# Second attention of a two-layer block: scores in two orientations instead of transposed exponentials

## The chip, the cores and the metric

The kernel runs on one core of a Trainium2 chip. The metric is device time in microseconds (us) of one execution; the time of a kernel is the median of its runs.

## What is computed

The block holds 16 sequences of 128 tokens with 256 features and runs two layers on them: a quantized attention, a gated feed-forward part (FFN), a second attention, and a mixture of experts (MoE). The change touches the second attention alone:

```
def _L1_xattn_ref(Q, K, V, attention_mask, w_q, w_k, w_v, w_o, b_o):
    q = (Q @ w_q.T).reshape(B, S, G, HG, HD)      # 8 groups x 4 heads, head size 8
    k = (K @ w_k.T).reshape(B, S, G, HD)
    v = (V @ w_v.T).reshape(B, S, G, HD)
    scores = jnp.einsum('bnghd,bmgd->bnghm', q, k) / scale
    scores = jnp.where(pad, NEG_INF, scores)      # masked keys
    scores = jnp.where(causal, scores, NEG_INF)   # keys after the query
    attn = jax.nn.softmax(scores, axis=-1)
    out = jnp.einsum('bnghm,bmgd->bnghd', attn, v).reshape(B, S, D)
    return out @ w_o.T + b_o
```

There are 32 heads of size 8; four heads share one key and value head. Softmax is taken with the row's maximum subtracted.

## The kernel before

The layers run one after the other, with some overlap at their borders. The second attention is the loop at the end of the listing below. It starts while the FFN's last four sequences are still being written (`down`), and it interleaves four kinds of side work: the input side of the next four sequences (`front_step`: load, normalize, transpose with `turn`, project with `qk`), `keys`, the output projection `output`, and the routing of finished tokens to experts (`route`, a generator of which each step runs one stage). The tile framework orders the instructions of each engine by dependency and priority, so side work lands between the attention's own instructions.

A step n of that loop handles one sequence b, one half c of the 256 features (16 heads) and one pair p of 32-row strips (8 heads). 64 steps make the stage; two steps with the same b and c are called a **pass** here, and there are 32 passes.

- `keys(b)`: GpSimd copies the keys four times, each copy zeroed except for the eight rows of one head (`kb`, line 975). The value heads are spread over 32-column slots (`vpad`, line 986).
- `scores(n)`: two matmuls with an identity put the mask into PSUM (line 997, bf16), and two matmuls of 32 rows each, one in each of two row strips of the array, add queries times keys (line 1004). The result has queries on partitions.
- `top(n)`: VectorE takes minus the maximum over the keys (line 1011).
- `exp(n)`: ScalarE takes eight exponentials of 128 x 128, one for each head, as the maximum is a bias per partition and differs between heads (line 1020).
- `probs(n)`: the values product contracts over keys, which must be on partitions. So TensorE transposes the exponentials (line 1031), and VectorE copies them out of PSUM (line 1032).
- `values(n)`, once per pass: 16 matmuls with the values and 16 with ones for the row sums (line 1047), each in one of four 32-column strips of the array; a reciprocal and a product on VectorE (lines 1053, 1054) give the output.

[...] Before, the stage has two score tiles of two banks, two banks for transposes (tag `tr`), one for everything else (tag `mm`: projections, `keys`, `output`, `down`, routing) and one for `values` (tag `pv`).

Of the kernel before, what the change touches and what calls it, by code (L numbers as in the profile page):

```python
# [9 lines left out]
F32 = mybir.dt.float32  # L10
# [3 lines left out]
I32 = mybir.dt.int32  # L14
AF = mybir.ActivationFunctionType
ALU = mybir.AluOpType
AX = mybir.AxisListType

P = 128
B = 16  # L20
# [15 lines left out]
def flamingo_kernel(  # L36
# [40 lines left out]
    def ps(tag, shape, bufs):  # L77
        return psum.tile(shape, F32, tag=tag, name=f"ps_{tag}", bufs=bufs)

    def ps_mm(shape):  # L80
        return ps("mm", shape, 2)

    def ps_tr(shape):
        return ps("tr", shape, 2)

    def ps_sc(shape):
        return ps("sc", shape, 2)
# [14 lines left out]
    def kpn(ap):  # L102
        return ap.rearrange("(k p) n -> p k n", p=P)
# [135 lines left out]
    with (  # L239
# [74 lines left out]
        class Unit:  # L314
# [198 lines left out]
            def probs(self, c):  # L513
                e, _ = self.e.pop(c)
                pt = ps_tr([P, 4, P])
                for j in range(4):
                    nc.tensor.transpose(pt[:, j, :], e[:, j, :], ident)  # L517
                eT = ap.tile([P, 4, P], F32, tag="eT", name="eT")
                nc.scalar.copy(eT, pt)  # L519
                self.eT[c] = eT  # L520
# [343 lines left out]
    ao = cq.tile([P, KD, DM], F32, name="ao")  # L864
    bo = cq.tile([P, DM], F32, name="bo")
    nc.sync.dma_start(out=aq, in_=kpn(aqT))
    nc.sync.dma_start(out=ak, in_=kpn(akT))
    nc.sync.dma_start(out=av, in_=kpn(avT))
    nc.sync.dma_start(out=ao, in_=kpn(aoT))
    nc.sync.dma_start(out=bo, in_=b_o.partition_broadcast(P))  # L870
# [8 lines left out]
        base=0, channel_multiplier=1,  # L879
    )  # L880

    hmask = cq.tile([P, NQ], F32, name="hmask")
    nc.vector.memset(hmask, 0.0)
    for q in range(P // 32):
        rows = hmask[32 * q : 32 * q + 32, :]
        nc.gpsimd.memset(rows, 1.0)
        nc.gpsimd.affine_select(
            out=rows, in_=rows, pattern=[[-HD, NQ]], compare_op=ALU.is_ge, fill=0.0,
            base=0, channel_multiplier=1,
        )  # L890
        nc.gpsimd.affine_select(
            out=rows, in_=rows, pattern=[[HD, NQ]], compare_op=ALU.is_ge, fill=0.0,
            base=HD - 1, channel_multiplier=-1,
        )

    ones8 = cq.tile([P, NQ, 32], F32, name="ones8")
    vpads = [cq.tile([P, NG, NQ, 32], F32, name=f"vpad{i}") for i in range(2)]
# [41 lines left out]
    def turn(g):  # L939
        y = front[g]["y"]  # L940
        hT = gp.tile([P, KD, NT], F32, tag="hT", name="hT", bufs=1)
        for k in range(KD):
            pt = psum.tile([P, G, P], F32, tag="tr", name="ps_tr", bufs=2)
            for j in range(G):
                nc.tensor.transpose(pt[:, j, :], y[:, j, k * P : (k + 1) * P], ident)
            nc.scalar.copy(hT[:, k, :], pt.rearrange("p n t -> p (n t)"))
        front[g]["hT"] = hT

    def qk(g, i, c):

        f = front[g]
        if c == 0:
            f[i] = gp.tile([P, KD, NT], F32, tag="qk"[i], name="qk"[i] + "T")
        w, src = ((aq, f["hT"]), (ak, f["cT"]))[i]
        pm = psum.tile([P, NT], F32, tag="mm", name="ps_mm")
        for k in range(KD):
            nc.tensor.matmul(
                pm, w[:, k, c * P : (c + 1) * P], src[:, k, :],
                start=(k == 0), stop=(k == KD - 1),
            )  # L960
        if i == 0:
            nc.scalar.activation(f[i][:, c, :], pm, AF.Copy, scale=SCALE1)
        else:
            nc.scalar.copy(f[i][:, c, :], pm)

    kbs, vps, es, eTs, oTs, scs, mxs = {}, {}, {}, {}, {}, {}, {}

    def keys(b):

        g, j = divmod(b, G)  # L970
        f = front[g]
        tok = slice(j * P, (j + 1) * P)
        kb = ap.tile([P, KD, NQ, P], F32, tag="kb", name="kb")
        for c in range(KD):
            nc.gpsimd.tensor_tensor(  # L975
                kb[:, c], f[1][:, c, None, tok].to_broadcast([P, NQ, P]),
                hmask[:, :, None].to_broadcast([P, NQ, P]), ALU.mult,
            )
        pm = psum.tile([P, NG, HD], F32, tag="mm", name="ps_mm")
        for k in range(KD):  # L980
            nc.tensor.matmul(
                pm, f["cT"][:, k, tok], av[:, k, :], start=(k == 0), stop=(k == KD - 1)
            )
        vp = vpads[b % 2]
        for i in range(NQ):
            nc.vector.tensor_copy(vp[:, :, i, HD * i : HD * i + HD], pm)
        kbs[b], vps[b] = kb, vp

    def scores(n):

        b, c, p = n // 4, n // 2 % 2, n % 2
        g, j = divmod(b, G)
        f = front[g]
        tok = slice(j * P, (j + 1) * P)
        s = psum.tile([P, 2, NQ, P], F32, tag="sc", name="ps_sc", bufs=2)
        for i in range(2):
            nc.tensor.matmul(
                s[:, i], identb, f["comb"][:, j, None, :].to_broadcast([P, NQ, P]),
                start=True, stop=False,
            )  # L1000
        with tc.high_priority(offset=100):
            for i in range(2):
                rows = slice(32 * (2 * p + i), 32 * (2 * p + i) + 32)
                nc.tensor.matmul(  # L1004
                    s[:, i], f[0][rows, c, tok], kbs[b][rows, c], start=False, stop=True
                )
        scs[n] = s

    def top(n):
        mx = small.tile([P, 8], F32, tag="mx8", name="mx8")  # L1010
        nc.vector.tensor_reduce(  # L1011
            mx, scs[n].rearrange("p i h t -> p (i h) t"), AX.X, ALU.max, negate=True
        )
        mxs[n] = mx

    def exp(n):
        s, mx = scs.pop(n), mxs.pop(n)
        e = ap.tile([P, 8, P], F32, tag="e", name="e", bufs=3)
        for i in range(8):
            nc.scalar.activation(  # L1020
                e[:, i, :], s[:, i // NQ, i % NQ, :], AF.Exp, bias=mx[:, i : i + 1]
            )
        es[n] = e

    def probs(n):
        e = es.pop(n)
        eT = ap.tile([P, 2, NQ, P], F32, tag="eT", name="eT", bufs=3)
        for i in range(2):
            pt = psum.tile([P, NQ, P], F32, tag="tr", name="ps_tr", bufs=2)
            for h in range(NQ):  # L1030
                nc.tensor.transpose(pt[:, h, :], e[:, NQ * i + h, :], ident)
            nc.vector.tensor_copy(eT[:, i], pt)
        eTs[n] = eT

    def values(n):

        if n % 2 == 0:
            return
        b, c = n // 4, n // 2 % 2
        if c == 0:  # L1040
            oTs[b] = ap.tile([P, KD, P], F32, tag="oT", name="oT")
        o = psum.tile([P, 2, P], F32, tag="pv", name="ps_pv", bufs=1)
        for t in range(2):
            for h in range(NQ):
                for q in range(4):
                    lhs = ones8[:, h, :] if t else vps[b][:, 4 * c + q, h, :]
                    nc.tensor.matmul(
                        o[32 * q : 32 * q + 32, t, :], lhs,
                        eTs[n - 1 + q // 2][:, q % 2, h, :],
                        start=(h == 0), stop=(h == NQ - 1),  # L1050
                    )
        r = ap.tile([P, P], F32, tag="rsum", name="rsum")
        nc.vector.reciprocal(r, o[:, 1, :])
        nc.vector.tensor_tensor(oTs[b][:, c, :], o[:, 0, :], r, ALU.mult)
# [29 lines left out]
    for g in range(B // G):  # L1084
# [3 lines left out]
        for b in range(g * G, (g + 1) * G):  # L1088
            down(b, hd, ps_pv([P, DM]) if b % 2 else ps_acc([P, DM]))
            if g == 1:  # L1090
                for i in range(3 * (b % G), 3 * (b % G) + 3):
                    front_step(0, i)
    psum0.close()
    act_set = nc.scalar.preload_act_table_set("natural_log_exp_and_others")
    tc.keep_in_program_order(act_set)
    f2 = ExitStack()
# [5 lines left out]
    )  # L1102


    N1 = 4 * B
    routes = []
    for n in range(-2, N1 + 5):
        if 0 <= n < N1:
            scores(n)
            top(n)  # L1110
        if 0 <= n - 1 < N1:
            probs(n - 1)
        if 0 <= n < N1:
            exp(n)
        if 0 <= n < G:
            down(B - G + n, hd, psum.tile([P, DM], F32, tag="mm", name="ps_mm"))
            if n == G - 1:
                tp.close()
                ep = ctx.enter_context(tc.tile_pool(name="e1", bufs=2, reuse_waits="tile"))
        if 0 <= n - 2 < N1:  # L1120
            values(n - 2)
        m = n + 2
        if m % 4 == 0 and 0 <= m < N1:
            keys(m // 4)
        g, i = divmod(n + 12, 16)
        if 1 <= g < B // G:
            front_step(g, i)
        for stages in routes:
            next(stages, None)
        m = n - 4  # L1130
        if m % 4 == 3 and 0 <= m < N1:
            output(m // 4)
            for b0, count in ROUTES:
                if m // 4 == b0 + count - 1:
                    routes.append(route(b0, count))
    for stages in routes:
        for _ in stages:
            pass
    f2.close()
    f1.close()  # L1140

    psum = ctx.enter_context(
        tc.tile_pool(
# [123 lines left out]
```

## Time and profile before

| | |
|---|---|
| median of 3 runs | 1544.2 us (1540.3 to 1545.12) |
| the profiled execution: time | 1540.11 us |
| the profiled execution: span of the trace | 1538.2 us |
| its mean granted TensorE clock | 0.968 |
| second attention, first mask matmul to last values matmul | about 1080 to 1389 us |
| first matmul of the MoE | 1411.87 us |

The profile gives, for each engine, its busy time; PE is TensorE's matmuls, PEld its weight loads, DVE is VectorE, ACT is ScalarE, POOL is GpSimd and SP issues DMAs. A matmul of fp32 data stands in the trace as two records, a transpose or a bf16 matmul as one. Records of matmuls overlap, since a new one starts while an earlier one drains, so the distance between the starts tells the cost and the duration of a record does not. Names such as L1004 are lines of the kernel before.

### The profile page before, as it was taken

The page shows a single profiled execution, that of the slowest core. Times are in us where ns is not written, and L with a number is a line of the kernel's source. Part 1 is how long each engine was busy: PE and PEld are TensorE (multiplying, and loading weights), DVE is VectorE, ACT ScalarE, POOL GpSimd, SP SyncE. Part 2 cuts the span into 40 slices and gives each one's busy share as a digit, 9 for nine tenths or more (in the row PEclk, how much of TensorE's full clock was granted, in tenths as well). Part 3 has the DMA queues.
Part 4 walks back from the last instruction along what each step waited for, and adds up shares of the span by engine and source line. Part 5 has one row for each costly group of instructions (what it writes and reads, how often), then busy time and mean ns, then how long its engine had stood idle before and what let it go on. Part 6 is the DMA issues. An engine that isn't in the chain of part 4 may idle for free. (4 is left out here: it accounts for less than half of the span.)

```text
span 1538.2 us, 24640 instructions
## 1 busy us (share of the span) xinstructions
PE 1388.1 (90%) x8612; PEld 1009.7 (66%) x8612; DVE 1052.2 (68%) x2788; ACT 814.6 (53%) x2421; POOL 669.5 (44%) x574
## 2 busy tenths in 40 slices
PE   2778889798897999999999986999999999996998
PEld 1567677677675677777777764555556666664887
DVE  8888878878789777676767765433579797883100
ACT  3656566566556676666666662353355454542121
POOL 4576666666766555556565554120021312111111
PEclk9799999999999999999999998999999999996999
DMA  4300000000013100000000003400210100001662
GB/s 122 112 7 18 28 11 32 15 11 22 11 45 100 44 23 22 11 19 15 18 15 18 8 8 110 141 1 0 83 49 9 50 9 36 9 36 63 194 198 67
DMA packets 51115, 68.67 MB, mean 45 GB/s; under 512 B 5291, under 2 KB 37739, under 8 KB 50992
## 3 DMA queue, kind: packets, MB, share of 16 engines
q1 hardware_dynamic: 36912, 41.31, 9.1%
q10 hardware_dynamic: 11456, 17.63, 3.6%
q0 software_dynamic: 2624, 8.16, 1.5%
q8 instruction: 68, 1.11, 0.3%
q14 instruction: 55, 0.45, 0.1%
HBM read 50.53 MB, written 16.81 MB: 44 GB/s over the span
## 5 line engine op out<-in xcount | busy, mean ns | idle before, releaser
L509 POOL TENSOR_TENSOR e<-e,sums 128x512 f32<-128x512 f32 x128 | 139.7, 1092 | 230.8 <-DVE sums L505 120.8
L497 ACT ACTIVATE e<-ps_sc,mx 128x128 f32<-128x128 f32 x512 | 181.3, 368 | 90.1 <-DVE mx L489 82.7
L454 POOL TENSOR_TENSOR raw<-raw,q_r 128x512 f32<-128x512 f32 x192 | 207.9, 1112 | 34.1 <-DVE q_r L180 33.0
L431 DVE BATCH_NORM_STATS2 q_st<-raw 128x6 f32<-128x128 f32 x768 | 174.1, 279 | 66.9 <-ACT raw L422 66.5
L1020 ACT ACTIVATE e<-ps_sc,mx 128x128 f32<-128x128 f32 x512 | 139.7, 384 | 119.1 <-DVE mx L1011 114.1
L565 PE MATMUL ps_acc<-wp,cat 128*128 128x512 f32 x512 | 160.4, 436 | 17.6 <-POOL cat L227 15.5
L463 PE MATMUL ps_tr<-ident,raw 128*128 128x128 f32 x768 | 121.9, 288 | 46.0 <-POOL raw L454 43.8
L227 POOL TENSOR_TENSOR cat<-e_t,e_e 128x1024 fp32r<-128x1024 bf16 x64 | 136.2, 2128 | 53.7 <-DVE e_t L221 52.1
L481 PE MATMUL ps_sc<-kT,qT 128*128 128x128 f32 x1024 | 140.3, 280 | 15.0 <-ACT qT L472 15.0
L481 PEld LDWEIGHTS ps_sc<-kT,qT 128*128 128x128 f32 x1024 | 131.1, 193 | 33.0 <-ACT qT L472 27.0
L463 PEld LDWEIGHTS ps_tr<-ident,raw 128*128 128x128 f32 x768 | 96.0, 147 | 83.3 <-POOL raw L454 58.2
L519 ACT COPY eT<-ps_tr 128x512 f32<-128x512 f32 x128 | 75.4, 589 | 139.0 <-PE ps_tr L517 138.9
L975 POOL TENSOR_TENSOR kb<-kT,hmask 128x512 f32<-128x512 f32 x32 | 33.6, 1067 | 243.9 <-PE ps_sc L1004 184.6
L565 PEld LDWEIGHTS ps_acc<-wp,cat 128*128 128x128 f32 x512 | 95.9, 194 | 57.4 <-POOL cat L227 22.2
L527 PE MATMUL ps_pv<-eT,vt 128*128 128x256 f32 x512 | 132.1, 379 | 1.0 <-DVE cat_y L538 1.0
L422 ACT COPY raw<-ps_mm 128x512 f32<-128x512 f32 x192 | 113.7, 593 | 27.9 <-PE ps_mm L410 24.8
L527 PEld LDWEIGHTS ps_pv<-eT,vt 128*128 128x128 f32 x512 | 95.9, 189 | 31.2 <-issue 9.0
L538 DVE TENSOR_TENSOR cat_y<-ps_pv,r_sm 128x512 bf16<-128x512 f32 x128 | 87.1, 680 | 39.7 <-PE ps_pv L527 39.5
L472 ACT ACTIVATE qT<-ps_tr,hv 128x512 f32<-128x512 f32 x128 | 100.9, 789 | 21.8 <-PE ps_tr L463 19.8
L497 ACT ACTIVATION_READ_ACCUMULATOR e<-ps_sc,mx 128x1 f32 x512 | 105.3, 206 | 0.0
L489 DVE TENSOR_REDUCE mx<-ps_sc 128x4 f32<-128x512 f32 x128 | 87.2, 681 | 23.6 <-PE ps_sc L481 23.6
L1011 DVE TENSOR_REDUCE mx<-ps_sc 128x8 f32<-128x1024 f32 x64 | 78.2, 1222 | 25.0 <-PE ps_sc L1004 23.4
(228 smaller groups left out, 2807.3 us busy)
## 6 DMA issues: line engine op xcount, KB each, us to landing
w1t<-in_w ACTq DMA_DIRECT2D x8, 1024.0 KB, 5.0
w2t<-in_w ACTq DMA_DIRECT2D x8, 1024.0 KB, 5.6
disp<-empty SPq DMA_DIRECT2D x16, 257.0 KB, 8.5
xe<-disp SPq DMA_DIRECT2D x8, 514.0 KB, 3.6
stage<-in_wprojT SPq DMA_DIRECT2D x16, 256.0 KB, 2.7
xg<-in_x SPq DMA_DIRECT2D x4, 512.0 KB, 3.9
xb<-in_x SPq DMA_DIRECT2D x16, 128.0 KB, 2.1
ctx<-in_ctxT SPq DMA_DIRECT2D x16, 128.0 KB, 2.2
```

The costliest lines, as they stand in the source:

```text
L227: nc.gpsimd.tensor_tensor(dst, t[:, part], e[:, part], ALU.subtract)
L422: nc.scalar.copy(raw.rearrange("p h d -> p (h d)"), pm)
L431: nc.vector.bn_stats(self.st[:, 4 * blk + j, :], self.raws[blk][:, j, :])
L454: nc.gpsimd.tensor_tensor(src, src, self.r[:, 4 * blk : 4 * blk + 4, None].to_broadcast([P, 4, P]), ALU.mult,)
L463: nc.tensor.transpose(pt[:, j, :], src[:, j, :], ident)
L472: nc.scalar.activation(dst, pt, AF.Identity, scale=hv[:, col : col + 1], bias=hv[:, col + 1 : col + 2])
L481: nc.tensor.matmul(pscore[:, j, :], qT[:, j, :], self.kT[:, 2 * c + j // 2, :], start=True, stop=True,)
L497: nc.scalar.activation(e[:, j, :], pscore[:, j, :], AF.Exp, bias=self.mx[:, j : j + 1], accum_out=sums[:, j : j + 1],)
L509: nc.gpsimd.tensor_tensor(e, e, sums[:, :, None].to_broadcast([P, 4, P]), ALU.mult)
L527: nc.tensor.matmul(pv[:, 2 * g : 2 * g + 2, :], self.vt[:, gg * P : (gg + 1) * P], eT[:, 2 * g : 2 * g + 2, :], start=True, stop=True,)
L565: nc.tensor.matmul(self.acc, self.cat[c // 2][:, h % 8, :], wpr[self.cross, c][:, j, :, :], start=(h == 0), stop=(h == 15),)
L1020: nc.scalar.activation(e[:, i, :], s[:, i // NQ, i % NQ, :], AF.Exp, bias=mx[:, i : i + 1])
```

## The change

A pass becomes a step of the loop (32 steps), and no exponentials are transposed. The scores are computed twice:

1. Queries on partitions, for the maxima only. All four row strips are used: 16 matmuls, each with one head's queries as the stationary operand (128 columns) and the keys as the moving one (128 columns). They contract over nine rows: eight features and one row that the second product needs.
2. The negated maxima are written into a tile `mx` at columns 0, 32, 64 and 96. Four transposes (`lift`) move them to the rows 0, 32, 64, 96, and VectorE adds that PSUM tile to the queries, which gives `qa`: each head's queries with minus its maximum in row 0 of the strip.
3. `flipped`: keys as the stationary operand with 1 in row 0 (`one_row`), `qa` as the moving one, 512 columns, one matmul in each row strip. The result has keys on partitions and the maximum already subtracted.
4. ScalarE takes two exponentials of 128 x 1024, with the key mask as bias. GpSimd sets the entries above the diagonal to 0 with `affine_select`, in place. `values` reads the result directly.

Queries reach the layout of one head per 32 rows through DRAM: `qk` writes them to `qd`, and `queries(b)` reads them back with eight DMAs of 16 KB per sequence. The score tiles become three (six banks), `values` keeps one, and all else, transposes included, shares the one remaining bank. `stay_after` fixes the order of some matmuls on TensorE and adds no semaphore.

```diff
+    nc.gpsimd.memset(ak, 0.0)
+    for k in range(KD):
+        nc.sync.dma_start(
+            out=ak[:, k].rearrange("p (g r) -> p g r", r=32)[:, :, 1 : 1 + HD],
+            in_=akT[k * P : (k + 1) * P, :].rearrange("p (g r) -> p g r", r=32)[:, :, :HD],
+        )
...
+    nc.sync.dma_start(out=maskc, in_=mask.rearrange("(b t) -> t b", t=P))
+    nc.vector.tensor_scalar(padc, maskc, 0.0, NEG, ALU.is_equal, ALU.mult)
...
+    q0s = [cq.tile([P, KD, NQ, P], F32, name=f"q0{i}") for i in range(2)]
+    mxs = [cq.tile([P, NQ, P], F32, name=f"mx{i}") for i in range(2)]
+    for t in q0s + mxs:
+        nc.gpsimd.memset(t, 0.0)
...
         if i == 0:
             nc.scalar.activation(f[i][:, c, :], pm, AF.Copy, scale=SCALE1)
+            nc.sync.dma_start(out=qd[g, c], in_=f[i][:, c, :])
         else:
-            nc.scalar.copy(f[i][:, c, :], pm)
+            nc.scalar.activation(f[i][:, c, :], pm, AF.Identity, bias=one_row)
...
+    def queries(b):
+        g, j = divmod(b, G)
+        for c in range(KD):
+            for q in range(4):
+                nc.sync.dma_start(
+                    out=q0s[b % 2][32 * q + 1 : 32 * q + NR, c],
+                    in_=qd[g, c, 32 * q : 32 * q + 32, j * P : (j + 1) * P].rearrange(
+                        "(h d) t -> d h t", d=HD
+                    ),
+                )
...
-        kb = ap.tile([P, KD, NQ, P], F32, tag="kb", name="kb")
-        for c in range(KD):
-            nc.gpsimd.tensor_tensor(
-                kb[:, c], f[1][:, c, None, tok].to_broadcast([P, NQ, P]),
-                hmask[:, :, None].to_broadcast([P, NQ, P]), ALU.mult,
-            )
...
+        s = [psum.tile([P, 2, NQ, P], F32, tag="sc", name="ps_sc", bufs=3) for _ in range(2)]
+        for q in range(4):
+            masks = nc.tensor.matmul(
+                s[q // 2][:, q % 2], identb,
+                f["comb"][:, j, None, :].to_broadcast([P, NQ, P]), start=True, stop=False,
             )
...
+            for h in range(NQ):
+                for q in range(4):
+                    rows = slice(32 * q, 32 * q + NR)
+                    ins = nc.tensor.matmul(
+                        s[q // 2][:, q % 2, h, :], q0s[b % 2][rows, c, h, :],
+                        f[1][rows, c, tok], start=False, stop=(h == NQ - 1),
+                    )
+                    stay_after(ins, masks)
...
+    def lift(n):
...
+        pt = psum.tile([P, NQ, P], F32, tag="mm", name="ps_mm")
+        for h in range(NQ):
+            nc.tensor.transpose(pt[:, h, :], mxs[n % 2][:, h, :], ident)
+        qa = ap.tile([P, NQ, P], F32, tag="qa", name="qa")
+        nc.vector.tensor_tensor(qa, pt, q0s[b % 2][:, c], ALU.add)
...
+    def flipped(n):
...
+        s = [psum.tile([P, 2, NQ, P], F32, tag="sc", name="ps_sc", bufs=3) for _ in range(2)]
...
+            for q in (2, 3, 0, 1):
+                rows = slice(32 * q, 32 * q + NR)
+                ins = nc.tensor.matmul(
+                    s[q // 2][:, q % 2], front[g][1][rows, c, j * P : (j + 1) * P], qa[rows],
+                    start=True, stop=True,
                 )
...
     def exp(n):
...
-        for i in range(8):
-            nc.scalar.activation(
-                e[:, i, :], s[:, i // NQ, i % NQ, :], AF.Exp, bias=mx[:, i : i + 1]
-            )
...
+        for s in fls.pop(n):
+            eT = ap.tile([P, 2, NQ, P], F32, tag="eT", name="eT", bufs=4)
+            nc.scalar.activation(eT, s, AF.Exp, bias=padc[:, b : b + 1])
+            flat = eT.rearrange("p q h s -> p (q h) s")
+            nc.gpsimd.affine_select(
+                out=flat, in_=flat, pattern=[[0, 2 * NQ], [1, P]], compare_op=ALU.is_ge,
+                fill=0.0, base=0, channel_multiplier=-1,
+            )
...
-    def probs(n):
...
-        for i in range(2):
-            pt = psum.tile([P, NQ, P], F32, tag="tr", name="ps_tr", bufs=2)
-            for h in range(NQ):
-                nc.tensor.transpose(pt[:, h, :], e[:, NQ * i + h, :], ident)
-            nc.vector.tensor_copy(eT[:, i], pt)
...
+    N1 = 2 * B
...
+    for n in range(-2, N1 + 4):
+        if 0 <= n < N1:
             scores(n)
             top(n)
         if 0 <= n - 2 < N1:
             values(n - 2)
+        if 0 <= n - 1 < N1:
+            flipped(n - 1)
+            exp(n - 1)
+        if 0 <= n < N1:
+            lift(n)
+        if n % 2 == 0 and 0 <= n + 2 < N1:
+            queries((n + 2) // 2)
+        if n % 2 == 0 and 0 <= n < N1:
+            keys(n // 2)
```

In the built program TensorE's order within a steady pass is: four mask matmuls, 16 scores, 16 values matmuls, four flipped, 16 matmuls with ones, four transposes of the maxima. Side work stands in between. A flipped tile of pass n-1 takes, in turn, a pair of banks that the scores of pass n have just left.

## The prediction

> **What bounds the kernel now.** I read the page's busy shares and slices first, then the windows over the second attention, then its groups, then its timeline.
>
> ```profile
> PE 1388.1 (90%) x8612; PEld 1009.7 (66%) x8612; DVE 1052.2 (68%) x2788; ACT 814.6 (53%) x2421; POOL 669.5 (44%) x574
> ...
> PE   2778889798897999999999986999999999996998
> ```
>
> PE is busy nine tenths of the span, and the slices 28 to 35 (1080 to 1390 us), the second attention, are full. A busy PE need not be at its peak, so the windows are next; after the range come the busy times of PE, PEld, DVE, ACT and POOL, and then the granted clock.
>
> ```profile
> 1200.00:1250.00 50.00, 50.00 (x518) 29.30 (x516) 39.33 (x81) 24.34 (x86) 14.07 (x13) 1.00 0.13 41
> ...
> 1300.00:1350.00 50.00, 49.86 (x595) 31.59 (x594) 43.00 (x91) 27.48 (x99) 7.15 (x7) 1.00 0.03 9
> ```
>
> In this stage DVE stands at 39 to 43 of 50 us, ACT at 24 to 27, POOL at 7 to 14: none is full, and the clock is. The groups between 1080 and 1390 us say what PE does:
>
> ```profile
> L1031 PE MATMUL ps_tr<-ident,e 128*128 128x128 f32 x512 | 79.9, 287 | 2.1 <-ACT e L1020 2.1
> L1004 PE MATMUL ps_sc<-kb,qT 32*128 32x512 f32 x256 | 72.1, 640 | 0.0
> L997 PE MATMUL ps_sc<-comb,identb 128*128 128x512 bf16 x128 | 38.7, 380 | 0.0
> L1047 PE MATMUL ps_pv<-eT,vpad 128*32 128x128 f32 x1024 | 38.6, 285 | 0.7 <-DVE eT L1032 0.7
> ```
>
> Their busy sums overlap and can't be added. The cost is the distance between starts, which the timeline gives (start, duration):
>
> ```profile
> 1314.51 1.13 PE L1004 MATMUL ps_sc<-kb,qT 32*128 32x512 f32 x4
> ...
> 1315.57 1.09 PE L1031 MATMUL ps_tr<-ident,e 128*128 128x128 f32 x8
> ...
> 1316.50 0.59 PE L997 MATMUL ps_sc<-comb,identb 128*128 128x512 bf16 x2
> ...
> 1317.03 1.13 PE L1004 MATMUL ps_sc<-kb,qT 32*128 32x512 f32 x4
> ...
> 1319.53 1.08 PE L1047 MATMUL ps_pv<-eT,vpad 128*32 128x128 f32 x32
> ...
> 1320.43 1.06 PE L1047 MATMUL ps_pv<-eT,ones 128*32 128x128 f32 x32
> ```
>
> PE goes from one kind to the next without a pause: scores at 1314.51, transposes at 1315.57, masks at 1316.50, scores at 1317.03. So a pair of scores takes 1.06 us with its change of array shape, eight transposes 0.93, a pair of masks 0.53, and the values 0.90 + 0.99 (the next masks start at 1321.42). A clean pass is 2 x (1.06 + 0.93 + 0.53) + 1.89 = 6.93 us. The starts of successive values groups are 7.4 us apart where only `keys` comes between, 8.4 with an output projection, 11 with front work. The stage (1080 to 1391 us) is 311 us: 32 x 6.93 = 222, side matmuls about 64 (estimated from their counts and spacing: 48 records of 512 columns at 0.43, 48 of `down` and 64 of `output` at 0.22, 160 small ones at about 0.11), and the other 25 are waits. Of these
>
> ```profile
>   PEld ps_tr L1031: 20.1, 28
> ```
>
> are transposes waiting for ScalarE's exponentials (20.1 us, 28 times). So the stage is bound by TensorE's own work, and what the change does there counts almost fully.
>
> **The change, part by part: TensorE.** fp32 matmuls cost two records. A record of 512 columns takes 0.43 us (L1004's two records in one strip start 0.53 apart, the first load of 0.107 among it), one of 128 a quarter, 0.107: the 32 values records, four strips side by side, follow each other at (1.08 - 0.28)/31 = 0.026, a quarter of that. So four column strips run at once, and L1004 shows two row strips at once (four records in 1.13 us).
> - Masks: four in a row, 0.53 + 2 x 0.215 = 0.96 (before 1.06).
> - Scores: 16 matmuls of 128 columns on four strips are 8 rounds of 0.107 = 0.86, plus the 0.2 for the shape that L1004 pays: 1.06. With a weight load at each, I take 1.10. Ends: 1.06, and 1.9 if no load hides (8 x (0.107 + 0.107) + 0.2).
> - Flipped: four matmuls of 512 columns on four strips, one L1004 step: 1.06; 1.92 if only two strips run at once.
> - Values: 1.89, and 0.1 for a shape change in their middle: 2.0.
> - Lift: four transposes, 0.54. The 16 transposes go (1.86).
>
> Sum 0.96 + 1.10 + 1.06 + 2.0 + 0.54 = 5.66 us against 6.93: 1.27 a pass, 41 us in all if nothing new waits.
>
> [...] The row is nearer: L1004's weights for its second record were loaded 0.107 us after the first ones, in the same strip, while the first record ran 0.43 us. I go by the row. [...]
>
> **The other engines, per pass.** DVE loses four copies of 0.68 and gains one add out of PSUM (nearest row: those copies, 0.68): from two reductions 2.44, copies 2.73, reciprocal 0.96, product 0.29 and some 1.9 of side work to about 6.3 us. ACT goes from 16 x 0.27 = 4.4 us to two exponentials of 1024 columns: 128 columns take 0.38 and 512 take 0.60 (L962), a Gelu of 256 takes 0.38; by the slope of the last two 1.04 each. POOL loses two `kb` products (1.07 each) and gains two selects, for which these are the rows:
>
> ```profile
> L887 POOL TENSOR_SCALAR_AFFINE_SELECT hmask<-hmask 32x4 f32<-32x4 f32 x4 | 0.8, 204 | 0.2
> L877 POOL TENSOR_SCALAR_AFFINE_SELECT causal<-causal 128x128 f32<-128x128 f32 x1 | 0.4, 361 | 0.0
> ```
>
> By the line through 4 and 128 columns (0.204, 0.361) a select of 1024 columns is 1.5 us; the 128-column rows span 0.36 to 0.39 and the small ones 0.18 to 0.20, which gives up to 1.7. If it went by elements alone it were 8 x 0.375 = 3.0; a memset of 1024 columns (1.05) is the lower end. I take 1.7.
>
> **New waits.** (1) In the built program, two of the flipped matmuls write the bank pair that the first reduction of the same pass frees. Scores end; 0.3 later the reduction starts and takes 1.22; the 16 values matmuls in between take 1.0. So two flipped strips start about 0.5 us late, unless side work stands there; behind them in PE's queue are the sums, the lift and the next masks. (2) The values need the selects: last flipped matmul, 0.3 of hand-overs, exponential 1.04, two selects, 0.1, then 0.9 of values and the next flipped 1.06 make a loop of 3.4 + 2 x 1.7 = 6.8 us. A pass with `keys` alone is 5.66 + 0.45 = 6.1, so the loop decides there (7.4 becomes 6.8), and hides wait (1); with an output projection it is 6.8 against 8.4; with front work PE decides, 10.0 against 11.3. (3) One bank for all side work: each tile holds it for its matmuls, some 0.3 of hand-overs and a copy of 0.4 to 0.7, with three to four tiles a pass; `turn` and `route` transposes no longer alternate between two. I allow 5 us. (4) Fill and drain: after the last scores, before needs 8.6 us to its last values (1380.1 to 1388.7); after it, reductions, lift, add, flipped, exponentials and selects follow for two passes, about 16. At the start `down` fills. I allow 8 us.
>
> Waits 1 and 2 come to 16 us over 32 passes, 3 and 4 to 13, shape changes around side work to 3; of the 25 us before, the 20 for exponentials go and 5 stay. Stage: 32 x 5.66 + 64 + 37 = 282 against 311: -29 us.
>
> **Cover.** Queries through DRAM: writes and reads of this kind landed in 1.7 to 2.0 us; `queries(b)` is issued two passes (16 us) ahead, eight issues of about 0.4 us on SP. The `out_x` stores stand in the same queue and wait for their rows (195.8 us in all before, harmless, nothing being behind them); now queries are behind them. The order puts each store after its row is due, so I cost it at 0; a store that came a pass late would cost up to 8 us once each. The first expert weights (2 x 1 MB) share the DMA engines then, 5 to 6 us each, within the lead. The finer loads of `ak` and `maskc`, and 4 us more memsets on POOL, happen around 950 to 990 us, and the first use is after 1003: 0, and at most 10 us if late.
>
> **Rivals.**
> [...]
> - B, *the banks*: the one side bank and the three rotating score tiles make PE wait 0.9 us more per pass, +29: 1543 us. For it: about two thirds of a pass has that bank taken, and after PE stands still the clock may drop (0.97 in one window). Against: the order sets other work between.
> - C, *GpSimd's select takes over, slower than before*: place, the select between exponential and values; price 3.0 us each. The loop is then 9.4 us in every pass, and the tokens' scatter (1 us each) and normalization (1.25 us each, 16 of them) on the same queue add about 0.4: 9.8 x 32 + 13 = 327 against 311, +16 to +18. It decides from 2.4 us per select, where 3.4 + 2A passes the mean pass of 8.2. For it: no row beyond 128 columns. 1558 us.
>
> **How the numbers follow.** The profiled execution took 1540.1 us, at the lower end of the runs shown; the median is 1544.2. -29 gives 1511 from the one and 1515 from the other: 1513. Chances: this 0.58 (its own range 1492 to 1530), A 0.12, B 0.12, C 0.18. 0.3% (4.6 us) is what a measurement here tells from no change. Faster: 0.58, most of A: 0.66; same: rest of A, part of B: 0.08; slower: C, most of B: 0.26. The range reaches down to 1490 (the 20 us of waits and the 41 us with little new) and up to 1557, near C.
>
> **What would show it.** [...] The forecast is wrong if four row strips don't run together, or if a select costs over 2.4 us.

## The result, and the profile after

The changed kernel takes 1556.2 us (median of 4 runs, 1553.5 to 1557.3) against 1543.6 in the same measurement: a ratio of 1.0082, 95% interval 1.0061 to 1.0103. It is slower, where 1513 and faster had been forecast. The profiled execution took 1553.45 us with a span of 1551.7, so 13.5 us more than the profiled one of before, and a mean clock of 0.950 against 0.968.

Two lines of the page after, from its busiest groups, show the two operations on the new path (count, then busy time in us, mean in ns):

```profile
L1086 POOL TENSOR_SCALAR_AFFINE_SELECT eT<-eT 128x1024 f32<-128x1024 f32 x64 | 69.2, 1103 | 233.1 <-ACT eT L1084 233.1
L1084 ACT ACTIVATE eT<-ps_sc,padc 128x1024 f32<-128x1024 f32 x64 | 68.1, 1110 | 172.0 <-PE ps_sc L1070 172.0
```

A select costs 1.10 us, less than the 1.7 assumed, and GpSimd mostly waits for ScalarE. A pass with no side work in it is as short as forecast; TensorE's timeline (start, duration):

```profile
1256.24 0.66 PE L1055 MATMUL ps_mm<-ident,mx 128*128 128x128 f32 x4
1256.73 1.03 PE L1027 MATMUL ps_sc<-comb,identb 128*128 128x512 bf16 x4
1257.69 1.17 PE L1035 MATMUL ps_sc<-kT,q 9*128 9x128 f32 x32
1258.79 1.08 PE L1103 MATMUL ps_pv<-eT,vpad 128*32 128x128 f32 x32
1259.80 1.50 PE L1070 MATMUL ps_sc<-qa,kT 9*128 9x512 f32 x8
1261.23 1.08 PE L1103 MATMUL ps_pv<-eT,ones 128*32 128x128 f32 x32
1262.24 0.44 PE L1055 MATMUL ps_mm<-ident,mx 128*128 128x128 f32 x2
```

From lift to lift it is 6.00 us, 0.37 of it a wait inside flipped, so 5.63 clean. Then where did the time go? The two traces, cut at the same events:

| stretch | before, us | after, us | difference |
|---|---|---|---|
| start to the last projection of the first attention | 947.6 | 950.1 | +2.5 |
| to the first masks of the second attention | 132.1 | 137.4 | +5.3 |
| to the start of the last scores | 299.3 | 284.9 | -14.4 |
| to the last values (drain) | 9.5 | 25.5 | +16.0 |
| to the first expert's transposes (tail) | 23.4 | 27.6 | +4.2 |
| experts | 126.3 | 126.1 | -0.2 |

For the second attention, first masks to last values (308.8 and 310.4 us; the last group isn't in the split), I took each group of matmuls against the short ones of its own form at full clock (20th percentile): what is over this in a stretch at half rate, up to half of that stretch, is charged to the clock, the rest to waits. This is a split by a rule of mine, not a reading of the profile.

| | before | after | difference |
|---|---|---|---|
| clean work | 286.8 | 255.5 | -31.3 |
| clock at half rate | 3.3 | 22.5 | +19.2 |
| waits | 17.9 | 31.7 | +13.8 |

The work did shrink. Most of what it gave went into the clock. The trace's record of the granted clock holds 47.8 us at half rate (a granted clock of 0.5) between first masks and last values, 6.8 before, always in multiples of 3.41 us (stretches of 3.41, 6.83 and 10.24). The windows of the changed kernel (after the range the busy us of PE, PEld, DVE, ACT, POOL; then the granted clock):

```profile
1090.00:1140.00 50.00, 47.38 (x532) 30.57 (x530) 25.50 (x43) 9.64 (x10) 13.32 (x12) 0.86 0.28 91
1140.00:1190.00 50.00, 49.75 (x713) 30.01 (x712) 32.70 (x65) 15.17 (x16) 13.77 (x13) 0.97 0.12 40
```

and of the kernel before:

```profile
1090.00:1140.00 50.00, 49.58 (x447) 28.45 (x447) 35.07 (x67) 21.98 (x78) 9.94 (x9) 1.00 0.30 97
1140.00:1190.00 50.00, 49.78 (x582) 30.78 (x580) 41.55 (x82) 26.74 (x95) 6.60 (x6) 1.00 0.03 11
```

In the first of the changed kernel, PE counts as busy for 47 of 50 us, and still it has only 0.86 of its clock.

### The profile page after: what moved, and what is told of

Its sections match the earlier page's. It is cut to its first block, busy times and chain, and to the rows that moved or that the text cites. A ratio compares the mean times of both kernels' runs of the same rounds, so it can differ in the third digit from the quotient of the medians.

```text
span 1551.7 us, 25619 instructions
## 1 busy us (share of the span) xinstructions
PE 1379.0 (89%) x9252; PEld 1006.7 (65%) x9252; DVE 1001.8 (65%) x2698; ACT 741.4 (48%) x1972; POOL 706.3 (46%) x599
## 2 busy tenths in 40 slices
DMA packets 61263, 72.76 MB, mean 47 GB/s; under 512 B 10571, under 2 KB 46859, under 8 KB 61136
## 5 line engine op out<-in xcount | busy, mean ns | idle before, releaser
L511 POOL TENSOR_TENSOR e<-e,sums 128x512 f32<-128x512 f32 x128 | 139.8, 1093 | 233.6 <-DVE sums L507 128.5
L499 ACT ACTIVATE e<-ps_sc,mx 128x128 f32<-128x128 f32 x512 | 180.9, 368 | 90.4 <-DVE mx L491 83.0
L1086 POOL TENSOR_SCALAR_AFFINE_SELECT eT<-eT 128x1024 f32<-128x1024 f32 x64 | 69.2, 1103 | 233.1 <-ACT eT L1084 233.1
L1084 ACT ACTIVATE eT<-ps_sc,padc 128x1024 f32<-128x1024 f32 x64 | 68.1, 1110 | 172.0 <-PE ps_sc L1070 172.0
```

What stands on the lines that cost most here:

```text
L499: nc.scalar.activation(e[:, j, :], pscore[:, j, :], AF.Exp, bias=self.mx[:, j : j + 1], accum_out=sums[:, j : j + 1],)
L511: nc.gpsimd.tensor_tensor(e, e, sums[:, :, None].to_broadcast([P, 4, P]), ALU.mult)
```

## The experiments

All are the changed kernel with one edit, unless said otherwise, measured beside the kernel before (medians 1541.1 to 1541.5 us). "Half-rate time" is that between first masks and last values.

### Rows of the strips

Scores and flipped contract over 9 rows of each strip of 32. The other rows hold zeros anyway.

```
-  rows = slice(32 * q, 32 * q + NR)
+  rows = slice(32 * q, 32 * q + 32)
```

> Edit: scores and flipped use all 32 rows of their strips, not 9; the added rows hold zeros, so the values are the same. [...] Theory 'pauses alone': the matmuls take as long as before and the half-rate time stays between 35 and 55 us; time within 3 us of 1556.

1542.7 us: 13.5 us less than the changed kernel by the medians, and some 10 us less by the ratios to before, from 1.0082 to 1.0015 (1.0004 to 1.0026), by an edit that adds multiplications by zero. Its windows over the same time:

```profile
1090.00:1140.00 50.00, 47.27 (x590) 30.60 (x593) 26.79 (x48) 12.26 (x13) 15.49 (x14) 1.00 0.30 97
1140.00:1190.00 50.00, 49.64 (x778) 31.19 (x771) 36.75 (x82) 16.13 (x21) 14.43 (x14) 1.00 0.12 39
```

PE's busy time is the same, the clock is full. By the split above: clean 256.1, clock 6.6, waits 33.3. So the waits were left as they were, and 16 us of clock came back. Half-rate time fell from 47.8 to 13.7 us; I had expected under 25, and "pauses alone" 35 to 55. That is one profile of each, but the mean clock of every run says the same: 0.947 to 0.951 in the four runs with 9 rows, 0.957 to 0.968 in the twelve with 32. So the rows counted, and "pauses alone" fell.

More doses follow: 20 rows, 28 rows, and 32 rows in one of the two kinds of matmul only.

> Edit: as the rows, but 20 rows of each strip instead of 32. [...] Rival 'any number below 32 is one case, a strip not fully used': as with 9 rows, 48 us and 1556. Rival 'it was the phase of the clock's windows that the rows run happened to hit': no order at all between 9, 20 and 32.

> Edit: 28 rows of each strip, the other parts as in the change. 20 rows left 44 us at half rate between first masks and last values, 9 rows 48, 32 rows 14. [...] Rival 'only a full strip counts': 40 to 50 us, time 1550 to 1557.

> Edit: 32 rows in scores alone, 9 in flipped. Both stream as many columns (16 matmuls of 128, 4 of 512). [...] Rival 'it is flipped's 9 rows' (long matmuls): as with 9 rows in both, 1553 or more. Rival 'it is the scores': as with 32 in both, within 2 us of 1542.7.

> Edit: 32 rows in flipped alone, 9 in scores. Theory 'flipped' (its four matmuls of 512 columns are the ones whose rows count): half-rate time between first masks and last values under 25 us and time within 3 us of 32 rows in both (1542.7). [...]

| rows in scores / flipped | half-rate time, us (one profile) | mean clock of a run (median of all runs) | time, us (median) |
|---|---|---|---|
| 9 / 9 | 47.8 | 0.949 | 1556.2 |
| 20 / 20 | 44.4 | 0.955 | 1550.1 (3 runs, 1545.6 to 1554.1) |
| 28 / 28 | 20.5 | 0.962 | 1542.7 |
| 32 / 32 | 13.7 | 0.964 | 1542.7 |
| 32 / 9 | 47.8 | 0.954 | 1554.7 |
| 9 / 32 | 23.9 | 0.958 | 1546.5 |

The mean clock is that of the whole execution, so it holds stretches outside the second attention too. Single profiles scatter: the other kernels with 9 rows below had 48 to 65 us at half rate, those with 32 rows 7 to 21, without overlap. So the order is clear, "only a full strip counts" fell with 28 rows, and the rival of the windows' phase, which asked for no order, fell with it. The shape of the dependence is not. By half-rate time 20 rows are nearly like 9 (just outside the 15 to 40 us that I had expected) and 28 like 32, which looks like a step; but the profile with 20 rows is of the slowest of its three runs, with the lowest clock (0.950; the others 0.955 and 0.957), and by the clock of all runs the rise is gradual.

Of the two kinds, flipped carries most. 32 rows there bring back 24 of the 34 us, as "flipped" expected, though the time stayed 3.8 us over 1542.7 where 3 had been allowed. 32 rows in the scores bring back none in this profile and no time, as "it is flipped's 9 rows" said, though the mean clock of its runs is a little higher. Both stream as many columns, so columns don't explain it; what does isn't known from these runs.

Are few rows enough? The kernel before, with 9 rows in its scores:

```
-  rows = slice(32 * (2 * p + i), 32 * (2 * p + i) + 32)
+  rows = slice(32 * (2 * p + i), 32 * (2 * p + i) + 9)
```

> Edit: the kernel before, with 9 of the 32 rows of each strip in its scores, so 23 of the 32 terms of each score are left out; the durations of its matmuls don't depend on that. Theory 'rows and pauses together' (few rows take away the reserve with which a window survives a pause): its passes pause little, so half-rate time between first masks and last values goes from 7 us to at most 25, time at most 10 us longer. Rival 'rows alone': most windows of the stage fall to half rate, over 100 us, time 40 us longer or more. Rival 'rows mean nothing in this kernel': 7 us, same time within 1.5 us.

1545.2 us (1.0019, 1.0003 to 1.0036), some 3 to 4 us longer, with 13.7 us at half rate for 6.8. In this kernel, which waits less (17.9 us by the split for the changed kernel's 31.7), few rows do little.

What pauses have to do with it is seen in the windows of 3.41 us. Call a pause what the distance between two starts on PE has over 0.43 us, a record of 512 columns. Of the changed kernel's 14 windows at half rate in the stage, 8 follow, at once or in a row, a window whose longest pause was 0.45 to 1.42 us, 4 one with a pause of 2.1 us or more, and 2 one in which the router's matmuls of 8 columns ran (16 records) without any pause. With 32 rows 4 are left, all behind pauses of over 1.7 us. The same count over the profiles of all five kernels with 9 rows and all five with 32, of windows in the stage that ran at full rate, each pause as far as it lies in its window:

| what the window held | 9 rows: next window at half rate | 32 rows |
|---|---|---|
| longest pause 0.4 to 1.5 us | 19 of 41 | 3 of 55 |
| longest pause over 1.5 us | 12 of 13 | 8 of 10 |
| most of the router's 16 records | 13 of 13 | 0 of 11 |
| none of these | 2 of 316 | 2 of 344 |

So few rows seldom halved the clock by themselves (2 of 316 windows). They lowered the pause that did (0.4 to 1.5 us: 19 of 41 for 3 of 55), and with them the router's matmuls became enough (13 of 13 for 0 of 11). (In the kernel before, with full rows, one of two windows with the router's matmuls was followed by half rate as well.) With 9 rows half a microsecond could be enough: 0.45 us was the shortest of these pauses in the changed kernel.

### DVE's queue and the front part

Two things were late that the forecast had costed at nothing or nearly so. First, the copy of the row numbers in `route` waits on DVE for an older route's scatter. `keys`' copies stand behind it, and the keys' projections need the bank that these free: PE stands idle there for 2.85 and 2.46 us.

```
-  nc.vector.tensor_scalar(keep, loc, float(CAP), None, ALU.is_lt)
+  kept = nc.vector.tensor_scalar(keep, loc, float(CAP), None, ALU.is_lt)
...
-  nc.vector.tensor_copy(row[:, :, 2 * DM + 1].bitcast(I32), number[:, gsl])
+  stay_after(
+      nc.vector.tensor_copy(row[:, :, 2 * DM + 1].bitcast(I32), number[:, gsl]), kept
+  )
```

> Edit: the copy of the row numbers in route is held behind that route's own slot arithmetic, so that DVE doesn't wait in it for an older route's scatter; nothing else. Theory 'DVE queue' (the two pauses of 2.6 and 2.2 us before the keys' projections come from keys' copies standing behind that copy, and each calls a half-rate window): both pauses gone, DVE's wait for scatters from 11.9 us to under 2, 6 to 9 us less time. Theory 'one side bank' alone: the projections still wait for the bank, pauses over 1 us stay, at most 2 us less.

1553.4 us. The wait for scatters left DVE's list and the two pauses left PE's, but nothing was gained: the ratio to the kernel before is 1.0083 (1.0066 to 1.0100), where it was 1.0082. By the split, waits fell by 5.7 us and the clock took 2.6 of them (25.1 for 22.5); that profile is of the fastest of four runs. Nor did each pause call a half-rate window, as I had expected: in the changed kernel only the first of the two was followed by one. On top of 32 rows:

> Edit: rows 32 and number late together. Theory 'few rows plus DVE queue' (the two are separate: rows bring the clock back, the copy behind a scatter makes pauses): the pauses of 3.1 and 2.8 us before the keys' projections, which the rows left, go; last scores 268 to 271 us after the first masks (274.4 with the rows alone, 282.5 with the late number alone), time 4 to 6 us under the rows alone. Rival 'the pauses only mattered through the clock': with the clock full they hide in later waits, within 1.5 us of the rows alone (1542.7).

1541.1 us, 1.6 less than with 32 rows alone, and 274.3 us to the last scores for 274.4: close to what the rival said. By themselves these pauses are not worth an edit. In the profiles with 20 rows and with the keys' weights in whole rows (below), which leave the copy as it was, both are gone, so they come and go with the scatter.

Second, the 5.3 us ahead of the first masks. The waits of the changed kernel from 945 to 1000 us (total, times, longest):

```profile
PE ps_acc L728 <- DVE hd L718: 3.4, 1, 3.4
...
DVE padc L898 <- DMA maskc<-in_mask: 2.5, 1, 2.5
DVE pad L925 <- DMA mi<-in_mask: 2.3, 2, 1.7
```

The kernel before, which has no mask columns, has this line there:

```profile
DVE pad L915 <- DMA mi<-in_mask: 3.0, 2, 1.6
```

DVE now waits for two masks, and behind these waits in its queue stands the product `hd` of the feed-forward part. PE waits 3.4 us for `hd`, and then a window of 3.41 us, from 985.9, runs at half rate. I moved the mask columns behind the feed-forward part:

```
-  nc.sync.dma_start(out=maskc, in_=mask.rearrange("(b t) -> t b", t=P))
-  nc.vector.tensor_scalar(padc, maskc, 0.0, NEG, ALU.is_equal, ALU.mult)
...
+  nc.sync.dma_start(out=maskc, in_=mask.rearrange("(b t) -> t b", t=P))
+  nc.vector.tensor_scalar(padc, maskc, 0.0, NEG, ALU.is_equal, ALU.mult)
   psum0.close()
```

> Edit: the load of the mask columns (2048 single elements) and the DVE operation on them are moved behind the feed-forward part; nothing else. Theory 'late mask' (the 137.4 us from the last matmul of the first attention to the first masks of the second, 132.0 before, are the wait of the feed-forward's product behind the mask on DVE, 3.4 us of PE, and the half-rate window after it): 131 to 133 us, time -5 us against the changed kernel (about 1551). Theory 'memsets and finer loads of the keys' weights': the 137 us stay, time within 1.5 us of 1556. Theory 'side bank': no effect here, within 1.5 us.

1557.2 us, 139.8 us to the first masks: nothing gained. DVE now waited 5.65 us for the row mask alone:

```profile
983.41 0.43 DVE L923 TENSOR_SCALAR pad<-mi 128x512 f32<-128x512 int32 x1 [5.65 <-DMA mi<-in_mask]
```

The suspect that is left stands ahead of it in SP's queue: the keys' weights, loaded in pieces of 32 bytes. So the next edit loads them in whole rows and spreads them on chip, with 32 rows and the mask columns late:

```
-  for k in range(KD):
-      nc.sync.dma_start(
-          out=ak[:, k].rearrange("p (g r) -> p g r", r=32)[:, :, 1 : 1 + HD],
-          in_=akT[k * P : (k + 1) * P, :].rearrange("p (g r) -> p g r", r=32)[:, :, :HD],
-      )
+  aks = cq.tile([P, KD, DM], F32, name="aks")
+  nc.sync.dma_start(out=aks, in_=kpn(akT))
...
+  if g == 1:
+      nc.gpsimd.tensor_copy(
+          ak.rearrange("p k (g r) -> p (k g) r", r=32)[:, :, 1 : 1 + HD],
+          aks.rearrange("p k (g r) -> p (k g) r", r=32)[:, :, :HD],
+      )
```

> Edit: rows 32; the keys' weights are loaded in whole rows as before the change, into a tile of their own, and spread to the strips on GpSimd; the mask columns are loaded after the row mask. Theory 'small packets' (4096 pieces of under 512 bytes, half of the keys' weights and half of the mask columns, hold up the row mask in the SP queue and in the DMA engines; with the mask columns moved alone the wait stayed at 5.7 us): DVE's wait for the row mask under 2.5 us, PE's pause in the feed-forward under 1.5 us (4.9 with the rows alone), 132 to 135 us from the first attention's end to the first masks, time 5 to 7 us under the rows alone. Rival 'memsets on GpSimd slow DVE's normalization': the 140 us fall by 2 at most.

1536.1 us (0.9966, 0.9953 to 0.9980), 6.6 less than with 32 rows alone. The packets under 512 bytes fell from 10571 to 8507, the way to the first masks from 140.2 (with 32 rows alone) to 133.0 us, and the same waits read:

```profile
DVE pad L920 <- DMA mi<-in_mask: 2.9, 2, 1.5
...
PE ps_acc L728 <- DVE hd L718: 0.6, 1, 0.6
```

PE's wait went from 4.5 us with 32 rows alone to 0.6. DVE's 2.9 us are over the 2.5 that I had expected, but they are those of the kernel before (3.0). "Small packets" held, and the weights were what counted: moving the mask columns alone had gained nothing.

### The drain

The last passes of the changed kernel on GpSimd, then on TensorE:

```profile
1375.16 0.97 POOL L847 DMA_INDIRECT disp<-row,slot_s  x1 [0.30 <-issue]
1376.14 2.15 POOL L1086 TENSOR_SCALAR_AFFINE_SELECT eT<-eT 128x1024 f32<-128x1024 f32 x2
```

```profile
1377.30 0.41 PE L1103 MATMUL ps_pv<-eT,vpad 128*32 128x128 f32 x4 [3.08 <-POOL eT L1086]
1378.34 1.92 PE L1103 MATMUL ps_pv<-eT,vpad 128*32 128x128 f32 x28 [0.62 <-POOL eT L1086]
1380.18 2.09 PE L1070 MATMUL ps_sc<-qa,kT 9*128 9x512 f32 x8
```

The selects stand behind the last of four scatters (the exponential was ready at 1371.3), PE waits 3.08 us for them, and then values and flipped take 1.92 and 2.09 us, where 1.08 and 1.14 are theirs at full clock: the granted clock was 0.5 from 1378.4 to 1385.2. Is the clock what makes the drain long? Fillers, matmuls that only keep TensorE busy, were to tell:

```
-  o = psum.tile([P, 2, P], F32, tag="pv", name="ps_pv", bufs=1)
+  o = psum.tile([P, 4, P], F32, tag="pv", name="ps_pv", bufs=1)
+  if n >= N1 - 3 or n < 0:
+      for _ in range(12):
+          nc.tensor.matmul(
+              o[:, 2:4, :], identb, front[g0(n)]["comb"][:, 0:2, :], start=True, stop=True
+          )
```

> Edit: ahead of the values of each of the last three passes twelve bf16 matmuls of 256 columns go into the unused half of the values' bank; nobody reads them. Theory 'clock' (in the drain, which takes 25.6 us from the last scores to the last values, the pauses halve the clock and so double values and flipped, 1.9 and 2.1 us where they take 1.08 and 1.14): they return to 1.1, the drain takes 20 to 22 us, time 3 to 5 us less. Theory 'latency' (the drain is the chain of exponential, select and values, in which the clock doesn't matter): the drain stays at 25 us or grows by the 1.3 us per filler, time 0 to 4 us more.

```profile
1398.37 1.08 PE L1111 MATMUL ps_pv<-eT,vpad 128*32 128x128 f32 x32
1399.38 1.14 PE L1073 MATMUL ps_sc<-qa,kT 9*128 9x512 f32 x8
```

The last two passes ran at full clock, yet the drain took 25.6 us and the kernel 1559.7, as "latency" had it. But this test is blunt: 6.8 of the drain's 13.7 us at half rate stayed, and the three fillers take 1.4 to 1.5 us each. With 32 rows, also with 6.8 us at half rate and without fillers, the drain took 22.4 us, so the clock does count for some 3 us of it. The other way is to shorten what is waited for (with 32 rows):

```
+  side = ["mm", 1]
...
-  lg = ps("mm", [P, G, NE], 1)
+  lg = ps(side[0], [P, G, NE], side[1])
...
+  yield
   for j, b in enumerate(bs):
...
+      stay_after(ins, last_select[0])
...
   for n in range(-2, N1 + 4):
+      if n > N1:
+          side[:] = tr_tag[:] = "sc", 3
```

> Edit: rows 32; the scatters of a route go behind the next pass's selects on GpSimd; from the last scores on, the output, the router's logits and transposes take the score banks, which are free then. Theory 'drain' (the 22.4 us from last scores to last values hold 3.4 us in which the selects stand behind four scatters and 1.9 us for the one bank, and the tail to the experts 27.3 us, 23.4 before the change, the rest for that bank): 17 to 19 us and 24 to 25 us, time 5 to 8 us under the rows alone. Rival 'latency of exponential, select and values': the drain stays above 21 us, time within 2 us.

(`pl` and the output's bank likewise; `last_select` is the last select issued.) 1535.1 us (0.9960, 0.9936 to 0.9983), 7.5 less than with 32 rows alone. The profiles show less: spans of 1535.5 and 1537.6, drain 21.7 for 22.4, tail 25.6 for 27.3. That of the rows alone lay 3.4 us under its median and this one 2.1 over. So the time followed "drain" and the stretch of that name followed "latency"; where the rest of the gain lies stays open. Together with the late copy and the front edit the drain came to 17.9 us, with 9 rows as with 32 (next table).

### All together, and all but the rows

> Edit: rows 32, front, drain and number late together. Theory 'separate costs' (clock, front, drain add up): 1542.7 - 6.6 - 7.5 - 1.5 = 1527, from 1524 to 1530, some 14 us under the kernel before; 132 to 134 us to the first masks, 272 to 275 to the last scores, under 22 to the last values, half-rate time in between under 14 us. Rival 'they share the same waits': 1532 to 1536.

> Edit: front, drain and number late, but 9 rows as in the change. Theory 'rows' (at 9 rows even the short pauses that are left halve the clock): half-rate time between first masks and last values stays over 28 us, time 1538 to 1545, at least 10 us over the version with all. Rival 'long pauses' (without the pauses over 2 us the clock would stay full with 9 rows too): under 15 us, time within 4 us of the version with all.

| | first masks, us | to last scores | drain | tail | half-rate time | median |
|---|---|---|---|---|---|---|
| before | 132.1 | 299.3 | 9.5 | 23.4 | 6.8 | 1541.1 |
| as changed | 137.4 | 284.9 | 25.5 | 27.6 | 47.8 | 1556.2 |
| all | 132.8 | 273.9 | 17.9 | 25.4 | 6.8 | 1530.3 |
| all but rows | 133.4 | 289.7 | 17.9 | 24.5 | 47.8 | 1546.0 |

(The row "as changed" is from the first measurement, with 1543.6 for the kernel before. The stretches and half-rate times are of one profile each.) All edits together give a version that is faster than both kernels: 1530.3 us, 0.9937 of before (0.9920 to 0.9955), 11 us under it where 14 were expected, just over the 1524 to 1530 of "separate costs" and under the 1532 of its rival. The same edits with 9 rows take 1546.0 (1.0044, 1.0020 to 1.0067): front and drain are as short, but the middle is 16 us longer, with 47.8 us at half rate for 6.8. Rival "long pauses" fell: at 9 rows the short ones and the router's matmuls do it too.

## Why the prediction was wrong

- **Term by term.** Forecast for the second attention, against the split of the result: passes -41 us against -38; side work +3 against +7; waits +9 against +14; the clock had no term, against +19. In sum -29 against +2. Another 12 us came ahead of this stage and behind it (2.5, 5.3 and 4.2), where next to nothing had been put.
- **The step that failed: "Stage: 32 x 5.66 + 64 + 37 = 282", summed at the full clock.** The first part says that "none is full, and the clock is", and carries this over to the new passes without a term for it. The matmuls of 9 rows were costed by their columns alone. At 9 rows the short pauses of the new passes and the router's matmuls halved the clock: 22.5 us for 3.3. With 32 rows in the same passes it is 6.6, and the time falls by 10 to 13.5 us. Rival B had "the clock may drop" after a pause, but as a side effect of the banks, and with no word of the rows.
- **The clean pass: right.** 5.66 us were worked out, 5.63 is what the pass above shows; over all passes scores, flipped, values, masks and lift come to 183.0 clean us, 5.72 each. The four row strips run at once and their weights are hidden: the scores' 32 records span 1.17 us, 1.10 from their first start to that of the next group, where 1.9 had been worked out for loads that don't hide. So L1004's row was the better guide, and rival A of the chances, loads not hidden, fell. No run shows the terms for changes of shape by themselves (0.2 us in scores and flipped, 0.1 in values, 3 around side work). Of the 0.2, 0.107 is the first weight load, by the prediction's own reading; in the pass above flipped took 1.06 us from start to start without its wait, and the values 1.01 + 1.01 where 0.90 + 0.99 stood before.
- **Side work: some 5 us too small.** 64 us and 3 for shape changes had been put in; its clean sum is 72.4 us, for 65.3 before.
- **The selects: mis-sized to the safe side.** 1.10 us for 1.7. Rival C, which asked for 3.0, fell, though its 1558 us lies near the result: the right time by the wrong mechanism. The forecast's range holds 1556.2 only because its upper end was put near C, so that is luck too. Values groups came 5.65 us apart without side work and 6.2 to 6.6 with `keys` alone, not 6.8.
- **Fill and drain: mis-sized.** The drain was put at "about 16" and took 25.5 us. Behind it are selects behind scatters (3.1 us of PE's wait), which rival C had named as 0.4 a pass, and waits for the one side bank. With 32 rows alone it was 22.4 us, with the queues mended 17.9, at 9 rows as at 32. By the split all waits come to 31.7 us, where the forecast had 34. So the other waits were fewer than put in, and the sum came out by errors that cancel, which is luck. (The 25 us of waits before were too many as well: 17.9 by the split.)
- **The side bank, costed within the second attention alone: 5 us.** The tail to the experts, where the router's transposes share that bank, grew by 4.2 us and had no term; with banks of its own 1.7 came back in one profile.
- **Cover: "0, and at most 10 us if late" for the finer loads. They were late:** 5.3 us, given back by whole rows. The end was right and the value was not: the first use was looked up on TensorE, after 1003, and not on DVE, where the mask's use stands in front of the feed-forward part's product, at 977 to 978 us of the trace of before. Queries through DRAM and the stores ahead of them cost nothing, as put: the list of waits has none of TensorE or VectorE for them.
- **Not of the change:** 2.5 us in the first attention, whose code is the same. A pause of 3.4 us at 908 to 909 us, found in both traces, was followed by a half-rate stretch of 6.8 us after and by none before. The end of that part lay between 945.5 and 952.7 us in the profiles of this study, with no order by edit, so these 2.5 us lie within its scatter.

## What to carry to other kernels

When a change makes matmuls narrower, in rows too, ask what happens to TensorE's clock and not only how many columns stream: zero rows that fill the strip cost nothing here and brought back 10 us or more. A clean pass time is worth only what the passes at both ends, and the windows at full clock, leave of it; look for the pauses that the new passes will have, and price each as itself and a window at half rate behind it (3.41 us here). And follow a "hidden" load to its first use on every engine (here DVE, where `hd` stood behind the mask), not to the use that you have in mind.

## What the hardware showed that was not expected

- The rows of a matmul mattered to the granted clock although they didn't to its duration: 9, 20, 28 and 32 rows gave 47.8, 44.4, 20.5 and 13.7 us at half rate, while at full clock the scores' 32 records span 1.17 us and flipped's 8 records 1.14 with 9 rows as with 32.
- With 9 rows, windows of 3.41 us with pauses of 0.4 to 1.5 us were followed by half rate in 19 of 41 cases, with 32 rows in 3 of 55. Router matmuls of 8 columns did it without a pause in 13 of 13 windows with 9 rows, and in 0 of 11 with 32.
- A load in pieces of 32 bytes, 2 x 32 KB, held up a mask of 256 KB behind it: its consumer waited 5.65 us with those loads ahead, 1.45 with whole rows.
- A select of 1024 columns on GpSimd takes 1.10 us, under two fifths of what eight selects of 128 columns would (8 x 0.36).
